# The first image's softmax in sixteen steps beside the second image's half of the position network

## The chip, the core and the metric

The kernel runs on one core of a Trainium2 chip. A core has engines that work side by side, each through its own queue of instructions in order: TensorE (PE in the profile; its weight loads are PEld), VectorE (DVE), ScalarE (ACT), GpSimd (POOL), and SyncE (SP), which issues most DMA transfers. TensorE writes to PSUM, eight banks of 2 KB for each of 128 partitions; the other operands lie in SBUF. The metric is device time in microseconds. Before the change it is 3857.22 us, the median of three runs (3856.22 to 3861.7).

## The reference

Four layers follow one another on two images of 512 channels and 32 x 32 pixels, all in float32. The change lies in the first, an attention with deformable keys. Each image has eight heads, and each head 1024 queries and 64 keys; the place of the keys is computed from the queries. A small network turns the distance between a query and a key into a bias:

```python
pos = grid_q[:, :, None, :] - grid_kv[:, None, :, :]
bias = jnp.sign(pos) * jnp.log1p(jnp.abs(pos))
bias = jax.nn.relu(bias @ cpb_w1 + cpb_b1)
bias = jax.nn.relu(bias @ cpb_w2 + cpb_b2)
bias = (bias @ cpb_w3 + cpb_b3).reshape(b, GROUPS, H * W, Hd * Wd)
sim = jnp.einsum('bhid,bhjd->bhij', qh, kh) + bias
attn = jax.nn.softmax(sim, axis=-1)
out = jnp.einsum('bhij,bhjd->bhid', attn, vh)
```

The network has 2 inputs, two hidden layers of 128 and one output, for 2 x 8 x 1024 x 64 pairs of query and key. It is most of the layer's work. An output projection with residual and a two-layer MLP with GELU close the layer. The other layers are a gated deformable convolution, a linear attention, and a full attention with group normalization.

## The kernel before

`biased_scores` (L821) runs the position network. It takes the sixteen heads of both images as eight pairs `p`; pairs 0 to 3 (`CC` is 4) belong to the first image and 4 to 7 to the second. For each pair the loop goes over `j` = 0, 2, ..., 30: 128 turns in all. A turn holds four groups `t`, each with two keys. For each key, `hidden` (L862) adds two precomputed terms on VectorE into a tile `h1` of 128 x 1024 and applies ReLU, thirteen times in sixteen on ScalarE (L871) and otherwise on VectorE (L869). `second_layer` makes two tiles `ph` from the two keys, each with eight calls of `matmul` on 32-column parts of the array (L882; each call appears twice in the profile), takes them from PSUM on ScalarE (L892, L894), and joins them on VectorE (L895). `last_layer` (L903) sums the last turn's four results into the PSUM tile `sim`, halfway through the following turn. Once per pair, `scores` (L915) adds the queries times keys to `sim`, and at the first turn of the next pair `store` (L925) writes it, with a bias, into `simT` in SBUF. Once per half pair, `first_layer` loads four tiles `ab` by DMA and scales them on ScalarE (L527).

Three buffers of two banks rotate as `ph` (tag "ph"), and one of two banks is `sim`; these are all eight banks. `h1` has six buffers. TensorE's instructions stay in the order in which the code writes them (`manual_schedule`). The order on the other engines is made by a scheduler, which takes an instruction when its inputs are ready in its own estimate, and among those that are ready the one written first.

The class `Softmax` (from L978) works on `simT`, which is keys by queries. `attention(p)` transposes it by eight 128 x 128 transposes (L986) into a PSUM tile `pt`, takes the maximum (L992) and subtracts it (L994) on VectorE, applies the exponential on ScalarE (L995), sums (L997), takes the reciprocal (L998) and multiplies (L999). `turn(p, e)` transposes the result back, eight transposes (L1006) into a PSUM tile `pb`, and ScalarE copies it over `simT` (L1011). `pt` and `pb` are taken from the `ph` buffers. In the kernel before, the softmax of pairs 0 to 3 is written after the loop: two attentions, the network's last `last_layer`, two more attentions, four turns, the last `store`. `image(1)` treats the second image's pairs later, woven into the first image's MLP.

After `biased_scores`, `projected` (L1034) forms values times the output weights, four pairs first, in banks that `ph` held. `project` (L1046) then multiplies these with the first image's softmax. The MLP of the first image (L1106, L1095) follows.

Of the kernel before, what the change touches and what calls it, by code (L numbers as in the profile page):

```python
# [10 lines left out]
F32 = mybir.dt.float32  # L11
# [7 lines left out]
CC = 4  # L19
HW = 1024  # L20
# [230 lines left out]
def chain(*parts):  # L251
    for part in parts:
        yield from part
# [23 lines left out]
def layers(net, out):  # L277
# [12 lines left out]
    with ExitStack() as later:  # L290
# [12 lines left out]
        with ExitStack() as l0a:  # L303
            l0a.enter_context(net.tc.manual_schedule(engines={mybir.EngineType.PE}))

            q_flat = new_room()[:, : (NP * 36 + 6) * 34]
            q_pad = q_flat[:, : NP * 36 * 34].rearrange("p (n y x) -> p n y x", y=36, x=34)
            keys = net.pool(l0a, "l0_k")
            kbd = keys.tile([128, NP, 128], F32, name="kbd", tag="kbd")
            dram = net.pool(l0a, "cpb_dram", space=bass.MemoryType.DRAM)  # L310
            feat = dram.tile([32, 2048], F32, name="feat_d", tag="feat_d")
            w2 = keys.tile([128, 128], F32, name="w2_t", tag="w2")
            first = net.pool(l0a, "cpb_ab", 4)
            parts = queries_keys_values(net, bn, simT, q_flat, q_pad, kbd, val, feat, first)
            nc.sync.dma_start(out=w2, in_=net.ins["w2"])

            def load_weights():
                t = new_room()
                w1 = t[:, : 4 * 2048].rearrange("p (k m) -> p k m", m=2048)
                out_w = t[:, 4 * 2048 :].rearrange("p (k m) -> p k m", m=C)  # L320
                nc.sync.dma_start(out=out_w, in_=net.ins["out_w"])
                nc.sync.dma_start(out=w1, in_=net.ins["mlp_w1"])
                return w1, out_w

            w1, out_w = biased_scores(
                net, q_pad, kbd, feat, w2, simT, first, parts, load_weights
            )
# [493 lines left out]
def biased_scores(net, q_pad, kbd, feat, w2, simT, first, parts, load_weights):  # L821
# [12 lines left out]
    with ExitStack() as ctx:  # L834
        small = net.pool(ctx, "cpb_w", 1)
        hid1 = net.pool(ctx, "cpb_h1", 6)
        lows = net.pool(ctx, "cpb_lo", 2)
        highs = net.pool(ctx, "cpb_hi", 6)
        ps_h = net.psum(ctx, "cpb_ps_h", 3)
# [6 lines left out]
        size = small.tile([128, 1], F32, name="size", tag="size")  # L846
# [51 lines left out]
        def last_layer(sim, j, sums):  # L898


            for n in range(2):
                for t in range(4):
                    nc.tensor.matmul(  # L903
                        sim[32 * t : 32 * t + 32, half(n)],
                        lhsT=w3[:, 30 - j : 62 - j],
                        rhs=sums[t][:, half(n)],
                        start=(j == 0),
                        stop=(j == 30),
                        skip_group_check=True,
                    )  # L910
# [13 lines left out]
        def store(p, sim):  # L924
            nc.vector.tensor_scalar(simT[:, p, :], sim, net.vec("cpb_b3"), None, ALU.add)  # L925

        pending = None
        sim = None
        hidden_done = 0
        for p, j in [(p, j) for p in range(NP) for j in range(0, 32, 2)]:  # L930
# [20 lines left out]
                if p == NP - 1:  # L951
                    weights = load_weights()
            pending = (p, j, sums)


        def two_banks(name):
            return ps_h.tile([128, HW], F32, name=name, tag="ph")

        def one(name, size):
            if size == HW:  # L960
                pool, tag = (hid1, "h1") if name == "e" else (highs, "hi")
                return pool.tile([128, HW], F32, name=name, tag=tag)
            return small.tile([128, size], F32, name=name, tag=f"soft_{name}", bufs=2)

        soft = Softmax(net, simT, one, two_banks)
        es = [soft.attention(p) for p in range(2)]
        last_layer(sim, *pending[1:])
        es += [soft.attention(p) for p in range(2, CC)]
        for p, e in enumerate(es):
            soft.turn(p, e)  # L970
        store(NP - 1, sim)
        return weights

# [1 line left out]
class Softmax:  # L975
# [4 lines left out]
        self.net, self.simT, self.one, self.banks = net, simT, one, banks  # L980

    def attention(self, p):
        nc, one = self.net.nc, self.one
        pt = self.banks("pt").rearrange("p (h j) -> p h j", j=64)
        for c in range(8):
            nc.tensor.transpose(  # L986
                pt[:, 2 * c : 2 * c + 2, :].rearrange("p h j -> p (h j)"),
                self.simT[:, p, 128 * c : 128 * c + 128],
                self.net.cst("ident"),
            )  # L990
        m = one("m", 16)
        nc.vector.tensor_reduce(m, pt, AX.X, ALU.max)  # L992
        e = one("e", HW).rearrange("p (h j) -> p h j", j=64)
        nc.vector.tensor_tensor(e, pt, m.unsqueeze(2).to_broadcast([128, 16, 64]), ALU.subtract)  # L994
        nc.scalar.activation(e, e, AF.Exp)  # L995
        s = one("s", 16)
        nc.vector.tensor_reduce(s, e, AX.X, ALU.add)  # L997
        nc.vector.reciprocal(s, s)  # L998
        nc.vector.tensor_tensor(e, e, s.unsqueeze(2).to_broadcast([128, 16, 64]), ALU.mult)  # L999
        return e  # L1000

    def turn(self, p, e):

# [1133 lines left out]
```

## Time and profile before

| quantity | value |
|---|---|
| median of three runs | 3857.22 us |
| profiled execution | 3854.95 us |
| its span, first to last instruction | 3853.2 us |
| TensorE busy | 3741.4 us (97%), 25356 matmuls |
| VectorE busy | 2768.0 us (72%) |
| ScalarE busy | 2567.4 us (67%) |
| mean granted TensorE clock | 0.990 |
| last second-layer matmuls begin (L882, block of 64) | 2095.27 us |
| first matmul of `projected` (L1034) | 2127.92 us |
| first matmul of `project` (L1046) | 2133.82 us |

The profile comes from one execution. Times in a timeline count from the start of its span. A timeline line gives the start, the duration, engine, line, operation, output and inputs, and how many instructions were merged; in brackets stands the idle time before it and what ended that. A group line gives the busy time and the mean of one instruction in ns, then the idle time just before. A line by stretch of time gives each engine's busy time, the TensorE clock that was granted, and the DMA share. Durations of neighbours can overlap: the time from start to start is what an instruction takes of its engine.

### The profile page before, as it was taken

How to read it: one execution, taken by the hardware profiler on the slowest of the kernel's cores; microseconds unless marked ns; L12 is line 12 of the kernel's file. 1: busy time of each engine (PE TensorE's matmuls, PEld its weight loads, DVE VectorE, ACT ScalarE, POOL GpSimd, SP SyncE). 2: the span in 40 equal slices, each digit the busy share in tenths (PEclk: the TensorE clock that was granted, in tenths of full speed). 3: DMA queues.
4: the chain of work that ended last, by engine and by line, in shares of the span. 5: the costliest groups of instructions: out<-in, count | busy, mean ns of one | idle time of the engine just before them, and what ended most of it. 6: DMA issues, size and time to landing. Idle time of an engine off the chain costs nothing. (4 is left out here: it accounts for less than half of the span.)

```text
span 3853.2 us, 59383 instructions
## 1 busy us (share of the span) xinstructions
PE 3741.4 (97%) x25356; PEld 1488.4 (39%) x25356; DVE 2768.0 (72%) x3242; ACT 2567.4 (67%) x2941; POOL 164.8 (4%) x180
## 2 busy tenths in 40 slices
PE   7999999999999999999999999999979989899999
PEld 4532232223222322222233444444434544455555
DVE  7999999999999999999999210411475563666565
ACT  7999999999999999999998221211123233345544
POOL 0000000000000000000000000000241240000000
PEclk9999999999999999999999999999999999999999
DMA  3000000000000000000011000122454471000000
GB/s 111 1 23 23 23 10 15 23 23 22 3 23 23 23 1 23 23 23 1 23 56 45 16 0 0 41 71 78 140 192 165 146 235 64 1 12 1 1 20 25
DMA packets 53883, 168.57 MB, mean 44 GB/s; under 512 B 4740, under 2 KB 10372, under 8 KB 50164
## 3 DMA queue, kind: packets, MB, share of 16 engines
q0 software_dynamic: 21776, 79.14, 6.4%
q1 hardware_dynamic: 31844, 85.63, 6.4%
q8 instruction: 200, 3.28, 0.4%
q14 instruction: 63, 0.52, 0.0%
HBM read 156.11 MB, written 8.65 MB: 43 GB/s over the span
## 5 line engine op out<-in xcount | busy, mean ns | idle before, releaser
L882 PE MATMUL ph<-h,w_t 128*32 128x512 f32 x16384 | 1797.2, 593 | 14.5 <-ACT lo L892 6.4
L862 DVE TENSOR_TENSOR h<-ab 128x1024 f32<-128x1024 f32 x1024 | 1206.4, 1220 | 73.6 <-PE ph L882 72.6
L882 PEld LDWEIGHTS ph<-h,w_t 128*32 128x32 f32 x16384 | 547.0, 110 | 1238.2 <-issue 1029.9
L871 ACT ACTIVATE h<-h 128x1024 f32<-128x1024 f32 x832 | 870.3, 1066 | 43.0 <-DVE h L862 40.8
L895 DVE SCALAR_TENSOR_TENSOR hi<-lo,low_w,hi 128x1024 f32<-128x1024 f32 x512 | 655.3, 1280 | 27.6 <-ACT hi L894 27.1
L894 ACT ACTIVATE hi<-ph,size_b,size 128x1024 f32<-128x1024 f32 x512 | 620.3, 1212 | 15.7 <-PE ph L882 10.2
L892 ACT ACTIVATE lo<-ph,vec_t 128x1024 f32<-128x1024 f32 x512 | 570.9, 1115 | 4.9 <-PE ph L882 4.9
L2059 ACT ACTIVATE e<-pl,m 128x1024 f32<-128x1024 f32 x128 | 143.5, 1121 | 226.6 <-DVE m L2051 226.6
L1540 PE MATMUL po<-fold,turned 128*128 128x512 f32 x576 | 270.7, 614 | 3.2 <-DVE dfacc L1548 2.9
L2051 DVE TENSOR_REDUCE m<-pl 128x1 f32<-128x1024 f32 x128 | 150.8, 1220 | 145.0 <-PE pl L1961 145.0
L1114 ACT ACTIVATE h<-ph,vec_t 128x512 f32<-128x512 f32 x64 | 44.0, 687 | 311.0 <-PE ph L1106 310.8
L903 PE MATMUL sim<-hi,w 128*32 128x512 f32 x2048 | 246.1, 592 | 0.6 <-DVE hi L895 0.6
L1487 DVE SCALAR_TENSOR_TENSOR sum<-got,wts,sum 128x256 f32<-128x256 f32 x432 | 187.2, 480 | 67.5 <-ACT sum L1483 64.1
L1106 PE MATMUL ph<-xn,room 128*128 128x512 f32 x512 | 230.2, 593 | 0.0
L1095 PE MATMUL acc<-h,mlp_w_t 128*128 128x512 f32 x512 | 229.8, 592 | 0.0
L1463 POOL DMA_INDIRECT got<-table,idx x144 | 150.2, 1043 | 590.8 <-DVE sum L1487 309.2
L2013 PE MATMUL pt<-cst_t,e 128*128 128x128 f32 x1024 | 148.2, 277 | 6.6 <-ACT aT L2024 4.0
L2013 PEld LDWEIGHTS pt<-cst_t,e 128*128 128x128 f32 x1024 | 117.9, 141 | 93.4 <-issue 61.1
L1540 PEld LDWEIGHTS po<-fold,turned 128*128 128x128 f32 x576 | 108.4, 198 | 115.6 <-issue 110.2
L1483 ACT ACTIVATE sum<-got,wts 128x256 f32<-128x256 f32 x106 | 53.2, 508 | 146.2 <-DMA got<-table,idx 128.0
L1095 PEld LDWEIGHTS acc<-h,mlp_w_t 128*128 128x128 f32 x512 | 97.3, 190 | 122.5 <-issue 122.0
L1106 PEld LDWEIGHTS ph<-xn,room 128*128 128x128 f32 x512 | 96.2, 190 | 117.2 <-issue 116.6
(250 smaller groups left out, 2702.5 us busy)
## 6 DMA issues: line engine op xcount, KB each, us to landing
ab<-feat_d SPq DMA_DIRECT2D x64, 512.0 KB, 4.7
room<-in_dc_w_dram SPq DMA_DIRECT2D x9, 1024.0 KB, 4.8
dc_w_t<-in_dc_w_dram SPq DMA_DIRECT2D x9, 1024.0 KB, 5.2
room<-in_mlp_w_dram SPq DMA_DIRECT2D x1, 4096.0 KB, 15.4
mlp_w_t<-in_mlp_w_dram SPq DMA_DIRECT2D x1, 4096.0 KB, 12.4
w_qkv_t<-in_w_qkv_dram SPq DMA_DIRECT2D x3, 1024.0 KB, 8.7
out_dram<-x_all SPq DMA_DIRECT2D x12, 256.0 KB, 2.0
got<-table,idx POOLq DMA_INDIRECT x144, 4.9
```

The costliest lines, as they stand in the source:

```text
L862: nc.vector.tensor_tensor(h1.rearrange("p (y x) -> p y x", x=32), at_x[:, k : k + 1, :].to_broadcast([128, 32, 32]), at_y[:, k, :].unsquee ...
L871: nc.scalar.activation(h1, h1, AF.Relu)
L882: nc.tensor.matmul(ph[32 * t : 32 * t + 32, half(n)], lhsT=w2[:, c0 : c0 + 32], rhs=pair[t // 2][:, half(n)], start=True, stop=True, skip_ ...
L892: nc.scalar.activation(lo, phs[0], AF.Relu, bias=b2_lo)
L894: nc.scalar.activation(hi, phs[1], AF.Relu, bias=size_b, scale=size)
L895: nc.vector.scalar_tensor_tensor(hi, lo, low_w, hi, ALU.mult, ALU.add)
L903: nc.tensor.matmul(sim[32 * t : 32 * t + 32, half(n)], lhsT=w3[:, 30 - j : 62 - j], rhs=sums[t][:, half(n)], start=(j == 0), stop=(j == 30 ...
L1095: nc.tensor.matmul(accs[oc], lhsT=self.w2[:, m, 128 * oc : 128 * oc + 128], rhs=hs[m], start=(m == 0), stop=(m == 15),)
L1106: nc.tensor.matmul(ph, lhsT=self.w1[:, k, 128 * m : 128 * m + 128], rhs=xn[:, k, :], start=(k == 0), stop=(k == CC - 1),)
L1487: nc.vector.scalar_tensor_tensor(t[:, q, :], g[:, s, :], w, t[:, q, :], ALU.mult, ALU.add)
L1540: nc.tensor.matmul(self.out, lhsT=turned[:, at : at + 128], rhs=self.folded.w[k][:, i, :], start=(k == 0 and i == 0), stop=(k == 8 and i = ...
L2013: nc.tensor.transpose(pt[:, 128 * c : 128 * c + 128], e[:, 128 * k : 128 * k + 128], ident)
```

## The change

The softmax of the first image moves into the turns of the loop that belong to the second image. `attention` is cut into three parts by `yield`, in a new generator `parts`; `steps(p)` runs these parts and then `turn`, so that a pair takes four steps and four pairs take sixteen. In every turn with `p >= CC` and `j % 8 == 4`, one step is issued at the end of the turn: in each pair's turns, `j` = 4 issues the transposes, maximum and subtraction, `j` = 12 the exponential and the sum, `j` = 20 the reciprocal and the product, and `j` = 28 the transposes back and the copy. The loop after it runs what is left (nothing is). The tiles `e`, `m` and `s` get a pool of their own with one buffer each; `pt` and `pb` are still taken from the three `ph` buffers. `attention` for the second image runs the same parts without a break.

```diff
+        exps = net.pool(ctx, "cpb_e", 1)
+
+        def two_banks(name):
+            return ps_h.tile([128, HW], F32, name=name, tag="ph")
+
+        def one(name, size):
+            return exps.tile([128, size], F32, name=name, tag=f"soft_{name}")
+
+        soft = Softmax(net, simT, one, two_banks)
+        beside = chain(*(soft.steps(p) for p in range(CC)))
+
         pending = None
...
             pending = (p, j, sums)
-
-
-        def two_banks(name):
-            return ps_h.tile([128, HW], F32, name=name, tag="ph")
-
-        def one(name, size):
-            if size == HW:
-                pool, tag = (hid1, "h1") if name == "e" else (highs, "hi")
-                return pool.tile([128, HW], F32, name=name, tag=tag)
-            return small.tile([128, size], F32, name=name, tag=f"soft_{name}", bufs=2)
-
-        soft = Softmax(net, simT, one, two_banks)
-        es = [soft.attention(p) for p in range(2)]
+            if p >= CC and j % 8 == 4:
+                next(beside, None)
+        for _ in beside:
+            pass
         last_layer(sim, *pending[1:])
-        es += [soft.attention(p) for p in range(2, CC)]
-        for p, e in enumerate(es):
-            soft.turn(p, e)
         store(NP - 1, sim)
         return weights
...
     def attention(self, p):
+        parts = self.parts(p)
+        for e in parts:
+            pass
+        return e
+
+    def steps(self, p):
+        for e in self.parts(p):
+            yield
+        self.turn(p, e)
+        yield
+
+    def parts(self, p):
         nc, one = self.net.nc, self.one
...
         nc.vector.tensor_tensor(e, pt, m.unsqueeze(2).to_broadcast([128, 16, 64]), ALU.subtract)
+        yield e
         nc.scalar.activation(e, e, AF.Exp)
         s = one("s", 16)
         nc.vector.tensor_reduce(s, e, AX.X, ALU.add)
+        yield e
         nc.vector.reciprocal(s, s)
         nc.vector.tensor_tensor(e, e, s.unsqueeze(2).to_broadcast([128, 16, 64]), ALU.mult)
-        return e
+        yield e
```

## The prediction

> **What bounds the kernel now.** I began with the costliest groups of the page, to see what the position network consists of, and then took the busy time of each engine in chosen stretches: one turn of its loop (eight second layers and one last layer) and three stretches of what follows the loop.
>
> ```profile
> L882 PE MATMUL ph<-h,w_t 128*32 128x512 f32 x16384 | 1797.2, 593 | 14.5 <-ACT lo L892 6.4
> L862 DVE TENSOR_TENSOR h<-ab 128x1024 f32<-128x1024 f32 x1024 | 1206.4, 1220 | 73.6 <-PE ph L882 72.6
> ```
> ```profile
> core 0: us, PE busy (x) PEld busy (x) DVE busy (x) ACT busy (x) POOL busy (x), PEclk, DMA share, GB/s
> 2064.40:2079.80 15.40, 15.40 (x148) 4.66 (x144) 14.51 (x14) 14.67 (x16) 0.00 (x0) 1.00 0.01 2
> 2106.00:2109.70 3.70, 3.66 (x26) 1.96 (x20) 3.70 (x4) 1.06 (x1) 0.00 (x0) 1.00 1.03 443
> 2113.00:2117.00 4.00, 1.86 (x8) 1.46 (x8) 4.00 (x5) 1.97 (x2) 0.00 (x0) 0.50 0.10 41
> 2128.00:2131.00 3.00, 3.00 (x4) 1.41 (x5) 0.00 (x0) 0.58 (x1) 0.96 (x1) 0.50 0.41 127
> ```
> TensorE is the bound of the loop: busy 15.40 of 15.40 us. VectorE (14.51) and ScalarE (14.67) are close behind, so a turn has 0.89 us of VectorE and 0.73 of ScalarE to give. VectorE's 73.6 us of idle time before L862 ends when TensorE has used an older h1, so VectorE runs ahead of TensorE and can lose a little without TensorE seeing it. After the loop VectorE becomes the bound (4.00 of 4.00), TensorE waits, and its granted clock falls to 0.50.
>
> The timeline of TensorE shows what extra ScalarE work costs inside the loop. One of these turns carries part of the four L527 activations of a half pair, and the store.
>
> ```profile
> 1354.73 1.90 PE L903 MATMUL sim<-hi,w 128*32 128x512 f32 x16
> 1356.45 5.33 PE L882 MATMUL ph<-h,w_t 128*32 128x512 f32 x48
> 1362.24 8.96 PE L882 MATMUL ph<-h,w_t 128*32 128x512 f32 x80 [0.46 <-ACT lo L892]
> 1371.02 1.90 PE L903 MATMUL sim<-hi,w 128*32 128x512 f32 x16
> ```
> From last layer to last layer this is 1371.02 - 1354.73 = 16.29 us; an ordinary turn is 15.45 (the next, 1371.02 to 1386.47). The turn before took 16.15. So four L527 at about 1.1 us of ScalarE, 4.4 us in some two turns, cost TensorE (16.29 + 16.15) - 30.90 = 1.54 us: the engine absorbs two thirds.
>
> The end of the loop, TensorE alone:
>
> ```profile
> 2095.27 7.05 PE L882 MATMUL ph<-h,w_t 128*32 128x512 f32 x64
> 2102.25 1.97 PE L986 MATMUL pt<-cst_t,simT 128*128 128x128 f32 x16
> 2104.15 1.06 PE L903 MATMUL sim<-hi,w 128*32 128x512 f32 x6
> 2105.86 1.90 PE L903 MATMUL sim<-hi,w 128*32 128x512 f32 x10 [0.65 <-DVE hi L895]
> 2107.69 1.97 PE L986 MATMUL pt<-cst_t,simT 128*128 128x128 f32 x16
> ...
> 2127.92 6.06 PE L1034 MATMUL pm<-room,val 128*128 128x512 f32 x8 [1.10 <-ACT simT L1011]
> 2133.82 1.53 PE L1046 MATMUL po<-simT,outv 128*128 128x512 f32 x3
> ```
> From the last hidden matmul (2102.2) to the first image's projection (2133.82) 31.6 us pass; L1034 starts only when the last softmax copy has freed its bank, and runs at half clock.
>
> **The change, part by part.** Sums are made against the profiled execution, 3854.95 us (span 3853.2 and 1.75 around it); the median of the runs shown is 3857.22, 2.27 above it.
>
> *Removed: the softmax after the loop.* What remains there: the last ScalarE activation L894 starts at 2102.39 and ends at 2103.59; L895, 1.27 us, follows in 0.04 and ends at 2104.90 (before, L992 stood ahead of it); the ten last matmuls L903 start 0.06 later and hold TensorE 1.83 us (2105.86 to 2107.69), to 2106.79. Then L1034: eight matmuls, which at full clock take 0.43 each (64 of L1046 in 27.55, from 2133.82 to 2161.37), 3.44 us, to 2110.2. Against 2133.82 that gains 23.6 us.
>
> Here a rule is weighed. TensorE: Matmul & The Clock Gate (What's actually happening) says that the clock halves after an idle window of about 3.4 us and needs as much busy time to come back. The row: 0.50 after the waits of 3.3 and 2.7 us between transposes, 6.06 us for L1034. What is left idle after the change is 1.7 us (2103.2 to 2104.96), so I take full clock; were it cold all the same, L1034 would keep its 5.9 us and the gain would be 21.1. The page's rule that speaks against the change is in Part 4: PE-mode transpose: transposes don't count as busy for the gate. If each of the eight groups of transposes put in the loop cooled it, with 3.4 us at half rate (1.7 lost) each, 13.6 us would go. In the profile the clock stays 1.00 from 2106.00 to 2109.70 with sixteen transposes in it; a group lasts 0.9 us among 60 us of dense matmuls, so I count nothing and keep 13.6 for the range.
>
> *Added: eight groups of eight transposes on TensorE inside the loop.* The page has this already once between dense matmuls, in the second image's softmax:
>
> ```profile
> 2175.44 1.04 PE L986 MATMUL pt<-cst_t,simT 128*128 128x128 f32 x8
> 2176.32 3.60 PE L1106 MATMUL ph<-xn,room 128*128 128x512 f32 x8
> ```
> 0.88 us from start to start, switch included; 1.90 / 2 = 0.95 after L882. I take 0.93: 8 x 0.93 = 7.4 us, paid in full since TensorE is the bound.
>
> *Added: a ph buffer taken out of the rotation of three.* Each pt holds one from its transposes until L992 and L994 have read it. With pt in its slot TensorE goes on with two ph (16 matmuls of four column tiles, 1.72 us each) and then wants pt's buffer, 3.4 us after the transposes. VectorE serves in order. The order at the same place of a turn in the loop (t = 3 ends at 1425.95):
>
> ```profile
> 1425.01 1.28 DVE L895 SCALAR_TENSOR_TENSOR hi<-lo,low_w,hi 128x1024 f32<-128x1024 f32 x1
> 1426.21 2.36 DVE L862 TENSOR_TENSOR h<-ab 128x1024 f32<-128x1024 f32 x2
> 1428.48 1.28 DVE L895 SCALAR_TENSOR_TENSOR hi<-lo,low_w,hi 128x1024 f32<-128x1024 f32 x1
> ```
> pt would be complete at 1427.0 and its buffer wanted at 1430.3. If L992 and L994 (1.15 each) go between the two L862 and ahead of L895, they end by 1429.7: no wait. If L992 comes after the second L862 and L895, L994 ends at 1432.0: 1.7 us of wait. In between (L992, L895, L994): 0.5. I take 0.7, four times: 2.8 us; ends 0 and 6.8. Behind L992 on VectorE stand the next L862, which may be late by up to 3 us; h1 has six buffers, and the L862 written at 1426.21 are for a pair that TensorE reaches some 8 us later, so that is absorbed.
>
> *Added: ScalarE and VectorE work in the loop.* Per pair of heads the exponential (0.95, back to back) and the copy L1011 (1.01) on ScalarE, and on VectorE 2 x 1.15 + 1.13 + 0.13 + 1.13 = 4.7 us. ScalarE: 8 operations at the L527 price, 1.54 / 4 = 0.38, are 3.1 us; as each copy comes with a pause of TensorE of 0.9 us, and an exponential that is ready early can fill an idle moment (0.73 per turn), I take half, 1.5; ends 0 and 3.1. VectorE: 18.8 us into 64 turns x 0.89 = 57 us of idle: nothing, held by the lead of h1; without that cover 18.8. The steps stand four turns (62 us) apart, and every wait of one step for the former is long over.
>
> *Moved: one table load.* ScalarE loads the exponential's table once, now at the first step. The row: 1.28 us at 2103.61, right behind the activation that ended at 2103.59. ScalarE: Activation LUTs (What ACT_TABLE_LOAD costs) adds a drain of 1.38 to it, 2.66 in all; the trace shows no such gap. At a third passed on, 0.5 us by the row, 0.9 by the rule; I take 0.5. No load back: at 3249.33 an exponential is followed by Identity at 3249.86 with no load between.
>
> *At nothing:* single buffers for e, m, s (reused 124 us later); the wrapper for the second image; all DMAs. SP's load of the MLP's second weights is issued at 2102.43, released by the network's last matmul, and lands 12.4 us later; first used at 2172.0, or 2148 after the change. The pad, off_w and taps work that waited for the last pb until 2126.9 comes earlier and is used past 2350. Later stages follow TensorE and shift as one block.
>
> Sum: 23.6 - 7.4 - 2.8 - 1.5 - 0.5 = 11.4 us. 3854.95 - 11.4 = 3843.6 for a profiled execution; 3857.22 - 11.4 = **3845.8 for the median**.
>
> **The rivals.**
> *Slower: pt's buffer.* One mechanism: VectorE's order puts L992 and L994 behind the hidden layer's work at each pt, and the lateness of h1 that follows stops TensorE again. Without any wait the change gains 23.6 - 7.4 = 16.2. It loses by more than 0.2% (7.7 us, about what a measurement of this kernel can tell from no change) if the waits sum to 23.9, 6.0 per pair. For: VectorE is 94% busy and in order. Against: its lead, and 1.7 us as the worst order that I find. At 7 us per pair: 3857.2 - 16.2 + 28 = 3869.
> *No difference.* Waits of 8.5 to 23.9 us, say each pt 1.7, ScalarE's 3.1 and half of a cold clock, 6.8, sum 16.7: 3857.
> *All absorbed.* Waits under 4 us: some 14 gained, 3843. For: the ordinary turns are exactly 15.45, with no wait at all, so that single operations vanish.
> *The gain is lost later*, because MLP weights or a gather set the pace: the 33 us in hand at L1095 speak against it; 3856.
>
> **How the numbers follow.** Likeliest (3844 to 3849.5): 0.40. All absorbed (below 3844): 0.22. No difference, 0.22, and lost later, 0.04: same 0.26. Slower: 0.12. Faster: 0.62. The range leaves out little below 3840 (16.2 gained is 3841) and about 0.1 above 3862.
>
> **What would show it.** Right: L1034 starts some 5 us after the last L882 and its eight matmuls take 3.4 us; turns with transposes for pt take 15.45 + 0.9 and up to 1.7 more, those for pb + 0.9; one table load before 2103 and granted clock 1.00 throughout. Wrong: L882 waiting on DVE e of L994 for more than 2 us a time, waits on h L862 in the turns after, a clock under 1.00 near the transposes, or table loads in pairs.

## The result

The changed kernel takes 3850.55 us (median of 10 runs, 3846.68 to 3857.92) where the kernel before, run beside it, takes 3859.07 (10 runs, 3853.53 to 3864.8): 8.5 us less, ratio 0.998 with a 95% interval of 0.9971 to 0.9988. The forecast was 11.4 us less. The profiled execution takes 3847.49 us, its span is 3845.7 against 3853.2.

In the changed kernel L999 are the transposes into `pt`, L1005 the maximum, L1007 the subtraction, L1009 the exponential, L1011 the sum, L1013 and L1014 the reciprocal and the product, L1021 the transposes into `pb`, L1026 the copy back, L1049 the values times output weights (L1034 before) and L1061 the projection (L1046 before).

**The end of the loop**, TensorE's timeline of the changed kernel, to be held against the lines of the same place shown in the prediction:

```profile
2109.39 7.05 PE L882 MATMUL ph<-h,w_t 128*32 128x512 f32 x64
2116.25 1.03 PE L903 MATMUL sim<-hi,w 128*32 128x512 f32 x6
2117.76 1.98 PE L1049 MATMUL pm<-room,val 128*128 128x512 f32 x4 [0.47 <-ACT hi L894]
2119.68 1.90 PE L903 MATMUL sim<-hi,w 128*32 128x512 f32 x10
2122.26 1.98 PE L1049 MATMUL pm<-room,val 128*128 128x512 f32 x4 [0.68 <-ACT outv L1050]
2124.07 2.39 PE L1061 MATMUL po<-simT,outv 128*128 128x512 f32 x5
```
From the last block of L882 to the projection 14.7 us pass (2109.39 to 2124.07) where 38.6 passed before (2095.27 to 2133.82). The wait for the last L895, which ten of the L903 need, is filled in part: half of the values' matmuls (L1049) stand ahead of these ten. But the block itself starts 14.1 us later than before. That is the price inside the loop.

**Engines by stretch of time**: 40 us of the loop around a `pt` group (its transposes start at 1398.82), the end of the loop, and what follows.

```profile
core 0: us, PE busy (x) PEld busy (x) DVE busy (x) ACT busy (x) POOL busy (x), PEclk, DMA share, GB/s
1380.00:1420.00 40.00, 39.84 (x369) 12.26 (x364) 39.67 (x37) 38.09 (x38) 0.00 (x0) 1.00 0.00 1
2116.00:2124.00 8.00, 6.85 (x29) 1.86 (x21) 2.57 (x2) 2.86 (x4) 2.02 (x1) 1.00 0.84 328
2124.00:2140.00 16.00, 16.00 (x38) 7.16 (x38) 4.10 (x6) 0.59 (x2) 0.00 (x0) 1.00 0.30 124
```
The granted clock is 1.00 in these stretches, and in every stretch of the loop (100 to 2107 us) as well; before the change it was 0.50 after the loop. And around a `pt` group VectorE is busy 39.67 of 40.00 us: there it has nothing left.

**Length of the loop.** In the rows of the tiles `sim` and `ph` the trace gives the start of the first last-layer matmul (L903) and of the last second-layer matmul (L882). Their distance is used below as the loop's length. The rows give these starts to 0.1 us, and so a length is good to 0.1. It is much more repeatable than the whole time: 2006.3 us in two profiles of the changed kernel. "Tail" is from that last L882 to the first projection matmul; "rest" from there to the end of the span. A turn, where one is named below, is timed from one first L903 to the next. Kernels for which no median is given ran once.

| kernel | loop | tail | rest |
|---|---|---|---|
| before | 1991.8 | 32.1 | 1719.4 |
| changed | 2006.3 | 8.3 | 1721.6 |
| changed, second profile | 2006.3 | 8.3 | 1717.5 |
| no first-image softmax | 1991.8 | 8.2 | 1721.7 |
| transposes only | 1999.2 | 8.2 | 1724.8 |
| exponential and product tied to their turns (pinned) | 2001.6 | 8.2 | 1722.6 |
| pinned, second profile | 2001.5 | 8.2 | 1721.9 |
| product alone tied | 2005.4 | 8.2 | 1720.0 |
| pinned, steps at 12, 18, 22, 28 | 2004.3 | 8.2 | 1724.8 |
| pinned, subtraction three times | 2013.7 | 8.2 | 1723.7 |
| changed, `e` in an h1 buffer | 2061.7 | 8.3 | 1723.4 |
| before, five h1 buffers | 2047.4 | 32.3 | 1722.1 |

The tail gains 23.8 us, the loop gives back 14.5. The rest, which no edit touches, varies by 7.3 us over these executions; so a difference of one or two microseconds between two single whole times says nothing about the change.

### The profile page after: what moved, and what is told of

Read it like the earlier page. It is cut to its first block, busy times and chain, and to the rows that moved or that the text cites. A ratio compares the mean times of both kernels' runs of the same rounds, so it can differ in the third digit from the quotient of the medians.

```text
span 3845.7 us, 59372 instructions
## 1 busy us (share of the span) xinstructions
PE 3740.0 (97%) x25356; PEld 1487.0 (39%) x25356; DVE 2768.3 (72%) x3242; ACT 2566.7 (67%) x2941; POOL 165.2 (4%) x180
## 5 line engine op out<-in xcount | busy, mean ns | idle before, releaser
L882 PE MATMUL ph<-h,w_t 128*32 128x512 f32 x16384 | 1807.8, 593 | 15.6 <-ACT lo L892 6.4
L862 DVE TENSOR_TENSOR h<-ab 128x1024 f32<-128x1024 f32 x1024 | 1206.4, 1219 | 67.1 <-PE ph L882 66.1
L882 PEld LDWEIGHTS ph<-h,w_t 128*32 128x32 f32 x16384 | 549.6, 110 | 1237.6 <-issue 1011.9
L895 DVE SCALAR_TENSOR_TENSOR hi<-lo,low_w,hi 128x1024 f32<-128x1024 f32 x512 | 655.2, 1280 | 31.3 <-ACT hi L894 30.0
L894 ACT ACTIVATE hi<-ph,size_b,size 128x1024 f32<-128x1024 f32 x512 | 620.8, 1212 | 16.8 <-PE ph L882 12.5
L892 ACT ACTIVATE lo<-ph,vec_t 128x1024 f32<-128x1024 f32 x512 | 571.4, 1116 | 5.8 <-PE ph L882 5.4
L903 PE MATMUL sim<-hi,w 128*32 128x512 f32 x2048 | 251.0, 592 | 0.0
```

The costliest lines, as they stand in the source:

```text
L862: nc.vector.tensor_tensor(h1.rearrange("p (y x) -> p y x", x=32), at_x[:, k : k + 1, :].to_broadcast([128, 32, 32]), at_y[:, k, :].unsquee ...
L882: nc.tensor.matmul(ph[32 * t : 32 * t + 32, half(n)], lhsT=w2[:, c0 : c0 + 32], rhs=pair[t // 2][:, half(n)], start=True, stop=True, skip_ ...
L892: nc.scalar.activation(lo, phs[0], AF.Relu, bias=b2_lo)
L894: nc.scalar.activation(hi, phs[1], AF.Relu, bias=size_b, scale=size)
L895: nc.vector.scalar_tensor_tensor(hi, lo, low_w, hi, ALU.mult, ALU.add)
L903: nc.tensor.matmul(sim[32 * t : 32 * t + 32, half(n)], lhsT=w3[:, 30 - j : 62 - j], rhs=sums[t][:, half(n)], start=(j == 0), stop=(j == 30 ...
```

## The experiments

**Without the softmax.** What is left when the first image's softmax is not computed at all (the projection reads scores that are not normalised):

```diff
-            if p >= CC and j % 8 == 4:
-                next(beside, None)
-        for _ in beside:
-            pass
```

> The changed kernel without the first image's softmax (none of its transposes, VectorE or ScalarE work; the projection reads scores that are not normalised). If the gain is the end of the loop alone and the rest is cost inside the loop: all turns of the second image as in the kernel before, the last block of second-layer matmuls (L882) at about 2095.3 us (2109.4 in the changed kernel), and the first projection matmul 14.7 us later, at about 2110. If instead part of the gain at the end hung on the new order of the loop, the distance from that block to the projection is not 14.7.

Loop 1991.8 us, to the tenth that of the kernel before, and the tail 8.2. The last L882 block starts at 2097.32 and not at 2095.3, as the loop of this execution began 2.1 us later. The projection comes 14.7 us after it (2112.01). So tail and loop are separate accounts: all of the tail's gain is due to the softmax being gone from there, and all of the 14.5 us in the loop to the softmax in it.

**Transposes alone.** VectorE's and ScalarE's part of the first image's softmax is left out:

```diff
+    def bare(self, p):
+        for name in ("pt", "", "", "pb"):
+            if name:
+                pt = self.banks(name)
+                for c in range(8):
+                    at = slice(128 * c, 128 * c + 128)
+                    self.net.nc.tensor.transpose(
+                        pt[:, at], self.simT[:, p, at], self.net.cst("ident")
+                    )
+            yield
```

> In the loop only the sixty-four transposes of the softmax, in their places; what VectorE and ScalarE do with them is left out, so the projection reads unnormalised scores. Theory (a group costs its own eight matmuls and two switches of the array's tiling, VectorE causes the waits two turns later): turns with a group last 16.6 us as in the changed kernel, all later turns 15.45, and the 0.8 and 0.45 us after the pt groups are gone; last L882 block at about 2103. Rival (waits for a PSUM buffer of the three are part of the 1.16 us): turns with a group last 16.3 to 16.4.

Loop 1999.2 us: the 64 transposes cost 7.4. A turn with a group lasts 16.61 us, 1.16 over 15.45; as nothing reads these tiles, no read buffer is part of it. Eight groups would be 9.3 us. Three of the four `pb` groups stand ahead of a turn in which the L527 activations make TensorE wait, and that turn falls from 16.15 to 15.45: TensorE's pause lets ScalarE catch up, which brings 2.1 us back. The theory held. The last block came at 2103.33 us, with a start 0.7 us later than in the kernel before; about 2103 was expected.

**The steps tied to their turns.** The exponential with the sum, and the reciprocal with the product, are queued behind the last L894 and L895 of the turn in which they are written. It changes the order on the two engines and nothing of the work.

```diff
-            nc.scalar.activation(hi, phs[1], AF.Relu, bias=size_b, scale=size)
-            nc.vector.scalar_tensor_tensor(hi, lo, low_w, hi, ALU.mult, ALU.add)
+            latest["act"] = nc.scalar.activation(hi, phs[1], AF.Relu, bias=size_b, scale=size)
+            latest["dve"] = nc.vector.scalar_tensor_tensor(hi, lo, low_w, hi, ALU.mult, ALU.add)
...
+        latest = {}
...
-                next(beside, None)
+                if j in (12, 20):
+                    with net.tc.issue_after(latest["act"].ins):
+                        with net.tc.issue_after(latest["dve"].ins):
+                            next(beside, None)
+                else:
+                    next(beside, None)
```

> The exponential with its sum, and the reciprocal with its product, are tied behind the last ScalarE and VectorE instruction of the turn in which they are written (j = 12 and j = 20), so that the scheduler can't pull them ahead. Theory (VectorE is late because 4.7 us of softmax fall into two turns): the waits of 0.8 and 0.45 us after each pt group vanish, the loop is 4 x 1.25 = 5 us shorter than the changed kernel's, last L882 block at about 2104.5, median about 3845.5. Rival (the 2.3 us of maximum and subtraction alone make VectorE late): the waits stay, last block at 2109. Second rival (pinned work hits its turn at a worse moment): as many waits, elsewhere.

First the changed kernel as it is. TensorE's timeline from the second pair's `pt` group on:

```profile
1398.82 1.10 PE L999 MATMUL pt<-cst_t,simT 128*128 128x128 f32 x8
1399.84 7.08 PE L882 MATMUL ph<-h,w_t 128*32 128x512 f32 x64
1406.73 1.90 PE L903 MATMUL sim<-hi,w 128*32 128x512 f32 x16
1408.45 11.33 PE L882 MATMUL ph<-h,w_t 128*32 128x512 f32 x100
1419.94 3.20 PE L882 MATMUL ph<-h,w_t 128*32 128x512 f32 x26 [0.16 <-DVE h L869]
```
The four `ph` after `pt` run without a break (1399.84 to 1406.73, 6.89 us). The wait comes a turn later: a hundred matmuls at 0.107 us end at 1419.2, and the next starts at 1419.94, when VectorE has delivered an h1 (the 0.16 in brackets counts from the modelled end of the last matmul). ScalarE and VectorE in the same stretch:

```profile
1404.68 1.04 ACT L1009 ACTIVATE e<-e 128x1024 f32<-128x1024 f32 x1
...
1418.18 1.06 ACT L871 ACTIVATE h<-h 128x1024 f32<-128x1024 f32 x1 [0.41 <-DVE h L862]
```
```profile
1400.10 1.22 DVE L1005 TENSOR_REDUCE m<-pt 128x16 f32<-128x1024 f32 x1
1401.23 1.28 DVE L895 SCALAR_TENSOR_TENSOR hi<-lo,low_w,hi 128x1024 f32<-128x1024 f32 x1
1402.42 1.22 DVE L1007 TENSOR_TENSOR e<-pt,m 128x1024 f32<-128x1024 f32 x1
...
1412.23 1.21 DVE L1011 TENSOR_REDUCE s<-e 128x16 f32<-128x1024 f32 x1
...
1428.75 1.23 DVE L1014 TENSOR_TENSOR e<-e,s 128x1024 f32<-128x1024 f32 x1
```
The steps are not four turns apart. The exponential, written four turns later, is issued 1.0 us behind the end of the subtraction; the sum follows in the same turn, and the product starts 30 us behind the transposes, not 124. From 1398 to 1432 us VectorE is never idle, while ScalarE waits for VectorE's sums (0.41 us in the line above): the early exponential is not what makes h1 late, VectorE is. The scheduler takes what is ready, and these were. The code spreads the steps for TensorE alone.

Tied, the same place of the loop looks like this on TensorE:

```profile
1399.35 1.10 PE L1005 MATMUL pt<-cst_t,simT 128*128 128x128 f32 x8
1400.38 7.07 PE L882 MATMUL ph<-h,w_t 128*32 128x512 f32 x64
1407.27 1.90 PE L903 MATMUL sim<-hi,w 128*32 128x512 f32 x16
1408.99 13.92 PE L882 MATMUL ph<-h,w_t 128*32 128x512 f32 x128
1422.72 1.90 PE L903 MATMUL sim<-hi,w 128*32 128x512 f32 x16
```
The 128 matmuls run through; the turn is 15.45 again. Of the four pairs only the first shows a new wait later on: the two turns around its exponential, the only one that loads the table, take 15.89 and 16.95 us, where the next two pairs have 15.45 and 15.96. The loop is 2001.6 us, 4.7 shorter than the changed kernel's, close to the 5 of the theory, and no wait of TensorE on VectorE's h1 is left in the second image's half. In the changed kernel the list of waits has them, four in number, at the weight loads and at the matmuls (columns: total us, times, longest):

```profile
PEld ph L882 <- DVE h L869: 4.8, 4, 1.6
PE ph L882 <- DVE h L869: 1.1, 4, 0.7
```
As to the whole time, the pinned kernel took 3844.83 us (10 runs) where the kernel before took 3857.32, ratio 0.9968 (0.9959 to 0.9978). It was run again beside the changed kernel:

> The pinned kernel once more, beside the changed kernel on the same chip. Its loop was 4.7 us shorter (2001.6 against 2006.3 us), the rest alike; if that is its whole difference, its median lies 4 to 6 us below the changed kernel's.

> The changed kernel once more, for the comparison with the pinned one: loop 2006.3 us, about 8.5 us below the kernel before. Loop lengths that differ from the first profile by more than 0.3 us would say that the loop is not as repeatable as taken.

There the pinned kernel took 3846.55 us (7 runs), the changed one 3847.9 (12), and the kernel before 3857.73: 1.4 us between the two, and not the 4 to 6 expected. Loop lengths repeated to 0.1 us; the profile of the changed kernel has by chance the shortest rest of all, 1717.5. That the loop is 4.7 us shorter is shown; that the whole kernel is faster than the changed one is not shown, since 1.4 us lies within the spread of these runs.

**The product alone tied.** Only the step at j = 20 is tied.

```diff
-                if j in (12, 20):
+                if j == 20:
```

> Only the reciprocal with its product is tied to its own turn; the exponential and the sum are free, as in the changed kernel. Theory (each piece of VectorE work that comes too early adds its own lateness): the first wait after a pt group (0.8 us) stays and the second (0.45 us) goes; loop 2004.5 us (changed kernel 2006.3, both tied 2001.6). Rival A (only the sum of all three crosses the limit): both waits go, 2001.6. Rival B (the reciprocal has no part): 2006.3.

Loop 2005.4 us, 0.9 under the changed kernel, and the four waits on h of L869 stay. The theory was right behind the group and wrong in the sum: the first wait stays, and the second goes (the turns of 15.88 and 15.91 us become 15.45). But most of it comes back in a later turn: the one that carries L527 takes 16.83 in place of 16.27 us, and in the last pair the one with L915 18.29 in place of 17.46. So 0.9 us were saved where 1.8 were expected, and tying the exponential and sum as well saves 3.8 more.

**The subtraction three times.** In the pinned kernel VectorE does the subtraction three times over in the loop, with the same result.

```diff
+    held = False
+
     def steps(self, p):
+        self.held = True
...
-        nc.vector.tensor_tensor(e, pt, m.unsqueeze(2).to_broadcast([128, 16, 64]), ALU.subtract)
+        for _ in range(3 if self.held else 1):
+            nc.vector.tensor_tensor(e, pt, m.unsqueeze(2).to_broadcast([128, 16, 64]), ALU.subtract)
```

> The pinned kernel with the subtraction (L994 of the kernel before) written three times, so that VectorE has 2.3 us more per pair in the turn of the pt group and pt keeps its PSUM buffer 2.3 us or more longer. If the three buffers are taken strictly in turn, TensorE waits at the third ph behind pt for all of it: loop at 2001.6 + 4 x 2.3 = 2011 us or more, with waits on the subtraction. If TensorE goes on with the two other buffers, there is no such wait, and what remains is VectorE's lateness, with about 4.6 us in one turn as much as in the changed kernel: waits on h1 of 0.5 to 1.3 us per pair, loop 2003.5 to 2007.

```profile
1402.02 1.10 PE L1008 MATMUL pt<-cst_t,simT 128*128 128x128 f32 x8
1403.05 7.07 PE L882 MATMUL ph<-h,w_t 128*32 128x512 f32 x64
1409.94 1.90 PE L903 MATMUL sim<-hi,w 128*32 128x512 f32 x16
1411.65 4.06 PE L882 MATMUL ph<-h,w_t 128*32 128x512 f32 x32
1416.16 1.05 PE L882 MATMUL ph<-h,w_t 128*32 128x512 f32 x4 [0.44 <-ACT h L871]
1418.20 1.06 PE L882 MATMUL ph<-h,w_t 128*32 128x512 f32 x8 [0.99 <-ACT h L871]
```
On VectorE an L862, the last subtraction, and the next L862:

```profile
1406.76 1.21 DVE L862 TENSOR_TENSOR h<-ab 128x1024 f32<-128x1024 f32 x1
...
1410.22 1.21 DVE L1017 TENSOR_TENSOR e<-pt,m 128x1024 f32<-128x1024 f32 x1
...
1413.15 4.62 DVE L862 TENSOR_TENSOR h<-ab 128x1024 f32<-128x1024 f32 x4
```
VectorE reads `pt` until 1411.4, and still four `ph` go through between 1403.05 and 1409.94 without a wait. TensorE runs on the other two buffers: the three are not taken strictly in turn. Yet the loop is 2013.7 us. By number alone that would be the first reading (2011 or more), but its sign is missing: no wait stands at the subtraction. The waits stand at h, where ScalarE's ReLU is late because VectorE has no L862 from 1406.76 to 1413.15. They cost 3.0 us per pair for 2.3 us of VectorE work; in the middle pairs 2.3 in the turn behind the group (17.75 in place of 15.45) and 0.7 in the turn with L527 (16.66 in place of 15.96). So my reading of the buffer was wrong, that of VectorE's lateness right, and its size (2003.5 to 2007) too small: here the extra VectorE work reached TensorE in full and more.

**Steps elsewhere.** Pinned, with the steps just ahead of the L527 turns:

```diff
-            if p >= CC and j % 8 == 4:
+            if p >= CC and j in (12, 18, 22, 28):
...
-                if j in (12, 20):
+                if j in (18, 22):
```

> The pinned kernel with the steps at j = 12, 18, 22 and 28 of each pair instead of 4, 12, 20 and 28. Both groups of transposes now stand just ahead of a turn in which ScalarE has its four L527, where TensorE waits 0.7 us in the kernel before. Theory (the pause that transposes make on TensorE lets ScalarE catch up, as in the run with transposes alone, where the turn after a pb group takes 15.45 in place of 16.15): the turn after a pt group takes 15.45 in place of 16.15 as well, about 0.7 us per pair; the loop, from the first last-layer matmul to the last second-layer matmul, is 1999 us where the pinned kernel has 2001.6 and the kernel before 1991.8; median about 3842. Rival (maximum and subtraction hit ScalarE's full turns, VectorE's results come later there): 2002 or more.

Loop 2004.3 us, 2.7 longer than pinned; median 3848.35 (9 runs), ratio 0.9973 (0.9963 to 0.9983). The rival was right that it doesn't pay, but the place is another. TensorE and ScalarE at a `pt` group:

```profile
1206.97 1.10 PE L1005 MATMUL pt<-cst_t,simT 128*128 128x128 f32 x8
1208.00 3.64 PE L882 MATMUL ph<-h,w_t 128*32 128x512 f32 x32
1212.14 3.64 PE L882 MATMUL ph<-h,w_t 128*32 128x512 f32 x32 [0.50 <-ACT lo L892]
```
```profile
1209.84 1.24 ACT L527 ACTIVATE ab<-ab,vec_t 128x1024 f32<-128x1024 f32 x1
1210.98 1.10 ACT L892 ACTIVATE lo<-ph,vec_t 128x1024 f32<-128x1024 f32 x1
```
The third `ph` behind the group waits 0.7 us for L892 (1208.00 + 3.44 = 1211.44 to 1212.14), as long as this turn waits in the kernel before. L892 stands behind an L527, so that the turn lasts 17.3 us, and the pause of the transposes is worth nothing. In the last pair, which has no L527 here, the same turn takes 16.61. Probably the buffer counts here, since `pt` holds one of the three; no run separates it from L527. And with two or three turns between the steps in place of four, those at 18 and 22 cost 0.67 and 0.55 us in turns that were 15.45.

**One h1 buffer less.** Two kernels: the changed one with `e` in one of the six h1 buffers, and the kernel before with five.

```diff
+            if name == "e":
+                return hid1.tile([128, HW], F32, name=name, tag="h1")
```

> The changed kernel with the tile e taken from the six h1 buffers, so that the network has five while e is alive. Theory (VectorE's lead in h1 buffers is what hides the softmax on VectorE): the lead shrinks by one tile of 1.13 + 1.06 us, and the waits after each pt group grow from 1.25 us to 3 or more; turns without softmax work get waits too if five buffers no longer carry the loop; last L882 block at 2115 or later. Rival (the lead has nothing to do with it): last block at 2109.4.

```diff
-        hid1 = net.pool(ctx, "cpb_h1", 6)
+        hid1 = net.pool(ctx, "cpb_h1", 5)
```

> The kernel before with five h1 buffers in place of six, nothing of the softmax moved. Theory (with e in an h1 buffer the loop lost 55 us in 64 turns because the network cannot run on five): every turn is longer, by about 0.9 us, 110 us in all, loop at about 2100. Rival (five are enough by themselves and only the softmax's VectorE work needed the sixth): loop at 1992.

The first takes 3905.59 us in its one run, loop 2061.7: 55.4 more than the changed kernel, all in the second image's half, 13.9 per pair. The second has a loop of 2047.4, 55.6 over the kernel before in twice as many pairs, 7.0 per pair (expected were 110 us in all). So five buffers are too few by themselves. But the first kernel's loss is not that of a shorter lead alone: up to 9.8 of its 13.9 us fall into one turn, that of the `pt` group, which takes 26.38 us in place of 16.61 (26.04 in the first pair). TensorE and VectorE there:

```profile
1420.98 10.01 PE L882 MATMUL ph<-h,w_t 128*32 128x512 f32 x64 [6.60 <-DVE h L869]
```
```profile
1414.41 1.22 DVE L1007 TENSOR_REDUCE m<-pt 128x16 f32<-128x1024 f32 x1 [1.92 <-PE pt L1001]
...
1417.88 2.35 DVE L862 TENSOR_TENSOR h<-ab 128x1024 f32<-128x1024 f32 x2
```
From 1404.4 to 1417.88 VectorE makes no h1, though it is idle for 6.2 us of it: in its order the next L862 stands behind the subtraction into `e`, and that has to wait for the transposes. Why the order is so was not tested. The two losses can't simply be divided into shares of the buffer and of the softmax.

## Why the prediction was right

It said faster by 11.4 us, with 3840 to 3862 as the range; measured were 8.5. The median, 3850.55, lies just above the band called likeliest (3844 to 3849.5), and the kernel before, run beside it, was 1.9 us above the figure that the forecast started from. By its steps:

- *The tail*: forecast 23.6 us, measured 23.8 (32.1 to 8.3). The path differed a little, as half of the values' matmuls were drawn ahead of the last ten L903. The clock stayed at 1.00 as I took it.
- *The clock near transposes*: 13.6 us were kept for the range, from the Trainium skill's rule in TensorE: Matmul & The Clock Gate (Part 4: PE-mode transpose) that transposes don't count as busy. The row from 1380 to 1420 us, with a group in it, has 1.00, so here nothing of it is due. A group of 1.1 us among dense matmuls does not put the rule itself to the test.
- *The transposes*: forecast 7.4 us, and 7.4 in the kernel with transposes alone, but as a sum of two errors. A group costs 1.16 and not 0.93. My row (0.88) stood between matmuls over the whole array, and my other figure (1.90 / 2) halved the edges along with the transposes. In the trace of the changed kernel the eight still follow each other every 0.11 us; what is added lies at the two edges, where the loop changes from 32-column parts to the whole array and back. That this change is the cause is likely, and no run separates it. Against that, 2.1 us came back, because a `pb` group relieves ScalarE's L527 turn. In the changed kernel itself only a third of this comes back: with the copy that follows `pb` that turn takes 15.90 us, where it is 15.45 with transposes alone and 16.15 before.
- *The buffer of* `pt`: 2.8 us at the third `ph`; measured none. The order L1005, L895, L1007 was the middle one of my three, but I took the buffers as strictly rotating, and the subtraction done three times shows that they are not.
- *VectorE, "nothing"*: this is the step that failed. I compared 18.8 us of work with 57 us of idle time over 64 turns, and took the steps as four turns apart. They run within two turns, the lead of h1 is used up there, and TensorE waits: in the three turns behind a `pt` group it loses 0.37, 0.43 and 0.46 us, 5.0 us in four pairs, and the loop is 4.7 us shorter once the steps are tied to their turns. Waits on h in the turns after were on my list of signs of being wrong, and they came.
- *ScalarE 1.5 and table load 0.5*: together 2.0; the pinned loop is 2.4 us above the one with transposes alone. About 1.35 of it are the copies (three turns of 15.90 in place of 15.45), and most of the rest is the table load, which only the first exponential has: in the changed kernel the turn with the first exponential takes 16.45 us where the other pairs have 15.82, 0.6 us more, and in the pinned kernel it is 1.4 over two turns.

One slip had no effect: `e` is written again four turns after its last reading, 67 us in the trace, and not 124 us.

Sum in the loop: forecast 12.2, measured 14.5. By turns, these are 9.3 for the eight groups, 5.0 behind the `pt` groups, 0.6 for the table load and 0.4 in the turns with L527 at the middle of a pair, less 0.8 behind the `pb` groups. That the sum came so near is in part luck: 2.8 us for a buffer wait that never came stand against 5.0 us that I had put at nothing. It leaves 9.3 us at the projection from loop and tail (9.7 in the profile, where the loop also began 0.4 earlier), and the rest of the program carried it on, give or take its own spread: 7.5 us less span in the profile, 8.5 in the medians.

## What to carry to other kernels

Writing a step later in the code moves only the engine whose order follows the code (here TensorE); where a scheduler fills in what is ready, the rest of the step runs early, so look in the trace for where it was issued, and tie it if the engine there is nearly full. Idle time counts where it lies: an engine that is 94% busy, as VectorE is here, takes extra work only out of its lead over the bound, and an average over 64 turns hides that. To judge a change inside a loop, measure the loop in the trace; here it repeats to 0.1 us while the rest of the program varies by 7.

## What the hardware showed that was not expected

- A group of eight transposes costs 1.16 us of a turn inside the loop of 32-column matmuls, where it takes 0.88 between matmuls over the whole array; the transposes themselves are 0.11 us apart in both.
- With transposes alone, a pause of 1.16 us on TensorE costs 0.46 net where it stands ahead of a turn in which ScalarE is overfull: that turn gets 0.70 us shorter. With a copy on ScalarE behind it, it gets only 0.25 shorter.
- One table load on ScalarE, 1.28 us long, costs the loop 0.6 us in the changed kernel and 1.4 in the pinned one, in which its place alone is another.
- In the kernel before, taking one of six buffers from the tile that VectorE feeds costs 55.6 us in 128 turns, though each engine's work per turn is the same.
